# Layer 1's end in a new order, with biases over 128 rows and one-hot masks on GpSimd

## The chip, the cores and the metric

The kernel runs on one core of a Trainium2 chip. The metric is the device time of one execution in microseconds; a kernel is told by the median of its timed runs. Five engines work beside each other, each in the order of its own instructions: PE (TensorE, products into PSUM), ACT (ScalarE), DVE (VectorE), POOL (GpSimd) and SP (which issues DMAs). They wait for each other by semaphores.

## The reference, cut to what matters

Four transformer layers, each an attention and a feed-forward part, run on 4096 rows of 128 numbers, all in fp32; each part works on layer-normed rows and its output is added to the rows. The change lies in the feed-forward part of layer 1:

```python
x1 = x @ sw1.T + sb1;  x2 = x @ sw2.T + sb2            # x: layer-normed rows, 64 wide out
sh = _ln(silu(x1) * x2, s_ln_g, s_ln_b)
shared_out = sh @ sw3.T + sb3                           # 128 wide out
x_moe = x[index_b, index_t]                             # 256 chosen rows
shared_scores = sigmoid(x_moe @ sg_w.T + sg_b)
expert_scores = sigmoid(x_moe @ eg_w.T + eg_b)          # 8 experts
top1_idx = argmax(expert_scores + exp_bias, -1)
top1_score = take_along_axis(expert_scores, top1_idx[:, None], -1)
weights = softmax(concatenate([shared_scores, top1_score], -1), -1)
h1 = einsum('md,ehd->meh', x_moe, ew1) + eb1
h2 = einsum('md,ehd->meh', x_moe, ew2) + eb2
z = _ln(silu(h1) * h2, sel_ln_g, sel_ln_b)
out_all = einsum('meh,edh->med', z, ew3) + eb3
expert_out = take_along_axis(out_all, top1_idx[:, None, None], 1)[:, 0]
final_out = shared_out.at[index_b, index_t].set(
    shared_out[index_b, index_t] * weights[:, :1] + expert_out * weights[:, 1:])
x = x + final_out
```

So all 4096 rows go through a shared expert, and 256 chosen rows get a weighted mix of the shared expert and the best of eight experts instead. Layer 2's attention follows at once, on the layer norm of these rows.

## The kernel before, in words

The rows are held on the chip as eight batches `x[0]` to `x[7]` of 512 rows, each 128 partitions x 4 tiles x 128 columns. Within a layer the order of the instructions on every engine is the order in which the program issues them; layer 1 writes that order out by hand.

Layer 1 first runs a loop over the batches with a list of stages, each with its own lag (`stages`), which brings attention for all batches up to batch 7 and the shared expert for batches 0 and 1. Then comes a straight list of calls, the end of layer 1, which the change rewrites. Its steps, per batch b:

- `f_stats(b)` (L885): mean and variance of the four tiles by DVE, the reciprocal root by three small POOL instructions (`stats_of` L700, `rstd_` L240). `f_scale(b)` (L888): ACT writes the normed rows `fxn` (two buffers), and SP writes them to DRAM (`by_rows`). `f_turn(b)`: four PE transposes, an ACT copy to `fxt`.
- `f_product(b)` (L913): products with `sw12` by `by_token` (L248), which adds the bias as one more product of `ones`, a single row, with the bias; ACT takes the tanh; `t[b]["gated"]()` is the DVE rest of the gate, giving `z`. `f_gate(b)` is both.
- `z_stats`, `z_scale`, `z_turn`: layer norm of `z`, transposed into `zts[b % 2]`.
- `z_out(b)`: products with `sw3`, then four DVE multiply-adds into `x[b]` with the mask `rest` (0 for chosen rows). `z_out_by_three(b)` (L950) does the same by PE, ACT (`zo`, one buffer) and a POOL add.

The 256 chosen rows go beside it, as two groups m: `chosen_biases` (L965) starts two pairs of PSUM banks with the experts' biases; `chosen_rows` (L971) gathers the rows from `by_rows` with two indirect DMAs of POOL, once all `by_rows` are written; `chosen_products`, `chosen_gates` (best expert as a one-hot `one`), `chosen_select` (L1037, the gate for all experts, times the one-hot, summed over experts), `chosen_norm`, `chosen_scale`, `chosen_affine`, `chosen_mix`, `chosen_turn`, and `chosen_out` (L1103), which gives `val`. `chosen_back` (L1132) writes `val` to its rows of the DRAM tensor `back` (zero elsewhere) with two indirect DMAs; layer 2 adds `back` to batches 1 to 7 later. For batch 0 there is no time for that: `put_rows(0)` (L760) makes one-hot matrices of the chosen positions, and `chosen_put` multiplies them with `val` and adds the product to `x[0]`. Then `x[0]` is normed (`stats_of`, `scaled`, `turned`) into `xt`, on which layer 2 starts (`queries(0)` in `late`).

`keep_clock(n)` (L769) is n products of the identity with itself, into a bank that nobody reads. Layer 2's first instruction on DVE writes `qb` into memory that layer 1's tiles had. PSUM in layer 1 is four single banks (`bank`) and two double ones (`bank2`), used in turn.

## Time and profile before

| | us |
|---|---|
| median of three timed runs | 1488.48 |
| lowest, highest of them | 1482.74, 1493.97 |
| the profiled execution | 1480.14 |
| its span, first to last instruction | 1478.4 |
| PE busy | 1402.5 (95%) |
| ACT busy | 1048.4 (71%) |
| DVE busy | 981.8 (66%) |
| POOL busy | 646.2 (44%) |
| mean granted clock of PE | 0.986 |

A row of the profile names the source line, the engine, the operation and the tiles (output, then inputs), how often it occurred and how long it took; the bracket at its end is how long the engine stood idle before it and which instruction of which engine it then followed. In rows of the timeline the first number is the start, in us from the start of the span. A `by_token` product is on line 246 for PE, as all products share that helper. The end of layer 1 lies from about 465 us (the last gather of attention) to 534 us (layer 2's first queries).

### The profile page before, as it was taken

The numbers are of one execution on the slowest core, as the hardware profiler recorded it, in microseconds if no ns is written. First come the engines' busy times: TensorE is split into PE (matmuls) and PEld (weight loads), VectorE is DVE, ScalarE is ACT, GpSimd is POOL, SyncE is SP. The second block draws the span as 40 slices with busy tenths as digits, with TensorE's granted clock in tenths as the row PEclk, the third lists the DMA queues.
The fourth block names the chain that finished last, engine by engine and source line by source line (L and its number), as shares of the span: only waits on it lengthen the run. The fifth ranks groups of instructions, "written<-read, shape, count | busy, mean of one in ns | idle before, by whom it ended". The sixth has DMA issues, their size and how long they took to land.

```text
span 1478.4 us, 22290 instructions
## 1 busy us (share of the span) xinstructions
PE 1402.5 (95%) x7766; PEld 673.5 (46%) x7766; DVE 981.8 (66%) x2049; ACT 1048.4 (71%) x2145; POOL 646.2 (44%) x744
## 2 busy tenths in 40 slices
PE   7789999999889889999999999999999999999996
PEld 3652222222376554443443445444445454454465
DVE  6766655675376638642673487786786777877876
ACT  7859899999776546664865585776876867668632
POOL 6647666665564333310530162452442623514423
PEclk9999999999999889999999999999999999999999
DMA  4049999898431011001000000000000000000000
GB/s 170 1 61 128 135 131 129 128 126 116 124 97 30 11 34 29 27 11 29 1 1 1 1 1 8 1 1 8 1 0 8 1 8 1 0 8 0 2 8 15
DMA packets 32897, 58.91 MB, mean 40 GB/s; under 512 B 5521, under 2 KB 25553, under 8 KB 28306
## 3 DMA queue, kind: packets, MB, share of 16 engines
q1 hardware_dynamic: 32080, 55.66, 21.5%
q8 instruction: 62, 1.02, 0.3%
q10 hardware_dynamic: 578, 1.57, 0.3%
q14 instruction: 49, 0.40, 0.1%
q0 software_dynamic: 128, 0.26, 0.1%
HBM read 49.18 MB, written 8.29 MB: 39 GB/s over the span
## 4 chain that ended last, share of the span: by engine, by line
PE 70%; ACT 18%; DVE 8%; issue 1%; POOL 1%; DMA 1%; POOLq 0%; DVEq 0%; ACTq 0%
PE ps L246 68%; ACT hm L555 8%; ACT hm L554 4%; ACT ex L1440 2%; DVE nm L1434 1%; DVE s L707 1%; DMA gates<-eq 1%; ACT xn L1356 1%; PE ps L1770 1%; POOL rs L243 0%; ACT h L376 0%; ACT xn L718 0%; DVE x L262 0%; PE ps L933 0%; DVE pr L567 0%
## 5 line engine op out<-in xcount | busy, mean ns | idle before, releaser
L1440 ACT ACTIVATE ex<-ps,nm 128x512 f32<-128x512 f32 x512 | 346.1, 688 | 183.4 <-DVE nm L1434 181.6
L1434 DVE TENSOR_REDUCE nm<-ps 128x2 f32<-128x1024 f32 x256 | 300.6, 1216 | 62.0 <-PE ps L246 61.4
L246 PE MATMUL ps<-q,k 64*128 64x512 f32 x1024 | 258.4, 621 | 5.6 <-ACT ex L1440 4.8
L246 PE MATMUL ps<-ex,vs 128*64 128x512 f32 x1024 | 233.8, 598 | 0.0
L573 POOL TENSOR_TENSOR acc<-acc,pr 128x512 f32<-128x512 f32 x119 | 166.4, 1398 | 110.0 <-DVE pr L567 102.3
L1455 POOL TENSOR_TENSOR vs<-v,sm 128x256 f32<-128x256 f32 x128 | 81.3, 635 | 295.9 <-DVE sm L1454 278.3
L555 ACT ACTIVATE hm<-ps,blob_f 128x1536 f32<-128x1536 f32 x128 | 196.3, 1534 | 0.0
L246 PE MATMUL ps<-xt,blob_a 128*128 128x512 f32 x304 | 151.4, 624 | 0.0
L246 PE MATMUL ps<-h,w 32*128 32x512 f32 x1024 | 148.9, 643 | 2.3 <-ACT xt L742 0.8
L567 DVE SCALAR_TENSOR_TENSOR pr<-ps,blob_f,gs 128x512 f32<-128x512 f32 x120 | 90.1, 751 | 91.0 <-PE ps L246 74.3
L246 PEld LDWEIGHTS ps<-q,k 64*128 64x128 f32 x1024 | 87.6, 187 | 137.7 <-issue 70.4
L246 PE MATMUL ps<-hm,w 128*32 128x512 f32 x1024 | 137.1, 607 | 3.5 <-DVE pr L567 3.4
L246 PEld LDWEIGHTS ps<-ex,vs 128*64 128x64 f32 x1024 | 67.8, 136 | 148.5 <-issue 131.1
L1642 POOL TENSOR_TENSOR acs<-acs,prod 128x512 f32<-128x512 f32 x98 | 124.7, 1272 | 10.7 <-ACT prod L1641 6.2
L242 POOL TENSOR_SCALAR rs<-mv 128x4 f32<-128x4 f32 (+1 forms) x69 | 17.9, 260 | 201.4 <-DVE mv L1346 140.8
L1440 ACT ACTIVATION_READ_ACCUMULATOR ex<-ps,nm 128x1 f32 x512 | 104.8, 205 | 0.0
L554 ACT ACTIVATE hm<-ps,blob_f 128x512 f32<-128x512 f32 x128 | 88.0, 688 | 19.1 <-PE ps L246 19.0
L246 PEld LDWEIGHTS ps<-xt,blob_a 128*128 128x128 f32 x304 | 52.9, 192 | 87.0 <-issue 62.1
L246 PEld LDWEIGHTS ps<-h,w 32*128 32x128 f32 x1024 | 41.1, 183 | 111.1 <-ACT hm L554 94.4
L1402 DVE TENSOR_TENSOR v<-ps,blob_bc 128x512 f32<-128x512 f32 x64 | 44.3, 692 | 67.5 <-PE ps L246 43.0
L246 PEld LDWEIGHTS ps<-blob_a,ct 128*128 128x128 f32 x512 | 67.0, 191 | 32.3 <-issue 29.2
L243 POOL TENSOR_TENSOR rs<-rs,half 128x4 f32<-128x4 f32 (+1 forms) x69 | 72.6, 1052 | 5.8
(296 smaller groups left out, 2206.9 us busy)
## 6 DMA issues: line engine op xcount, KB each, us to landing
gs<-gates SPq DMA_DIRECT2D x256, 128.0 KB
blob_f<-in_f SPq DMA_DIRECT2D x1, 2560.0 KB
blob_a<-in_a SPq DMA_DIRECT2D x1, 2056.0 KB
x<-in_x SPq DMA_DIRECT2D x8, 256.0 KB
gates<-eq SPq DMA_DIRECT2D x8, 256.0 KB
by_rows<-fxn SPq DMA_DIRECT2D x8, 256.0 KB
ge<-gates SPq DMA_DIRECT2D x4, 512.0 KB
back<-nought SPq DMA_DIRECT2D x7, 256.0 KB
```

The lines of the kernel that those rows point to most:

```text
L242: nc.gpsimd.tensor_scalar(t, var, EPS, None, ALU.add)
L243: nc.gpsimd.tensor_tensor(t, t, half[:, : t.shape[-1]], ALU.pow)
L246: nc.tensor.matmul(out_, lhs, rhs, start=start, stop=stop)
L554: nc.scalar.activation(hm[:, 0, :], p1, AF.Gelu, bias=bias)
L555: nc.scalar.activation(hm[:, 1:, :], p3, AF.Gelu, bias=bias)
L567: nc.vector.scalar_tensor_tensor(pr, po, f0["b2"][:, e : e + 1], gs, ALU.add, ALU.mult)
L573: nc.gpsimd.tensor_tensor(acc[:, b, :], acc[:, b, :], pr, ALU.add)
L1402: nc.vector.tensor_tensor(v, pv, bias, ALU.add)
L1434: nc.vector.tensor_reduce(nm, ps, AX.X, ALU.max, negate=True)
L1440: nc.scalar.activation(ex[kt][:, i, :], ps[:, i, :], AF.Exp, bias=nm[:, i : i + 1], accum_out=sm[:, kt, i : i + 1],)
L1455: nc.gpsimd.tensor_tensor(vs[:, tiles, :, :], vs_[n][:, tiles, :].rearrange("p j (i n) -> p j i n", i=2), sm[:, tiles, :].unsqueeze(3).to_ ...
L1642: nc.gpsimd.tensor_tensor(t["acs"], t["acs"], p, ALU.add)
```

## The change

It does five things. The bias of `sw12` and the biases of the experts are multiplied with `top_row`, a 128 x 128 matrix with ones in its first row and zeros below, instead of the single row `ones`; the experts' biases are loaded onto all 128 partitions (`ebs`) for it. The last `f_scale` writes its four tiles to DRAM one by one. `put_rows` and the multiplication by the one-hot in `chosen_select` are done by POOL; one of the two `zte` copies is done by DVE. `z_out_by_three` returns its POOL add for a later call and has two `zo` buffers; batches 6 and 7 use `z_out` again and batch 2 `z_out_by_three`. And the straight list has a new order, in which the shared expert of batches 5 to 7 lies between the steps of the chosen rows, with one `keep_clock(4)` in place of four calls with 5, 8, 10 and 6.

```diff
-    def by_token(terms, bias, width=D, tiles=J):
+    def by_token(terms, bias, width=D, tiles=J, by=None):
...
-            mm(pv, ones, bias.unsqueeze(1).to_broadcast([1, tiles, width]), start=False, stop=True)
+            n = bias.shape[0]
+            mm(
+                pv,
+                ones if by is None else by,
+                bias.unsqueeze(1).to_broadcast([n, tiles, width]),
+                start=False,
+                stop=True,
+            )
...
             def f_scale(b):
-                scaled(t[b]["fxn"], x[b], t[b]["fby"], J)
-                nc.sync.dma_start(
-                    by_rows[b * TB : (b + 1) * TB, :].rearrange("(j p) d -> p j d", p=P), t[b]["fxn"]
-                )
+                n = 1 if b == NB - 1 else J
+                to = by_rows[b * TB : (b + 1) * TB, :].rearrange("(j p) d -> p j d", p=P)
+                for j in range(0, J, n):
+                    scaled(fxn, x[b], t[b]["fby"], j + n, j)
+                    nc.sync.dma_start(to[:, j : j + n, :], fxn[:, j : j + n, :])
...
-                zo = wp.tile([P, J, D], F32, tag="zo", name="zo", bufs=1)
+                zo = wp.tile([P, J, D], F32, tag="zo", name="zo")
...
-                nc.gpsimd.tensor_tensor(x[b], x[b], zo, ALU.add)
+                return lambda: nc.gpsimd.tensor_tensor(x[b], x[b], zo, ALU.add)
...
-                    for k, name in enumerate(("eb1", "eb2")):
-                        mm(c_["two"][m][:, k, :], ones, rows[name], stop=False)
+                    for k in range(2):
+                        mm(c_["two"][m][:, k, :], top_row, ebs[:, k, :], stop=False)
...
-            def chosen_select(m):
+            def chosen_select():
...
-                nc.vector.tensor_tensor(s3, s3, one, ALU.mult)
+                    nc.gpsimd.tensor_tensor(s3, s3, one, ALU.mult)
...
-                    nc.scalar.copy(zte, pt)
+                    (nc.vector.tensor_copy if m else nc.scalar.copy)(zte, pt)
...
+                nc.gpsimd.memset(top_row, 0.0)
+                nc.gpsimd.memset(top_row[:1, :], 1.0)
+                for k, name in enumerate(("eb1", "eb2")):
+                    lo, hi = spans["rows"][name]
+                    nc.sync.dma_start(ebs[:, k, :], dram["rows"][:, lo:hi].partition_broadcast(P))
```

The straight list after the change (where `chosen_out` is cut into `chosen_shared_out`, `chosen_products_out` and `chosen_out`, and `chosen_put` into its product and its addition; `addN` is the POOL add that `z_out_by_three` returned):

```python
gather(7) f_stats(5) output(6) z_scale(1) attend(7) f_stats(6) f_gate(2) turn_o(7) f_scale(5)
z_turn(1) output(7) f_stats(7) f_scale(6) f_turn(5) f_scale(7) z_out(1) z_stats(2)
put_rows(0, POOL) chosen_rows() chosen_biases() f_turn(6) f_gate(3) z_scale(2) z_stats(3) f_turn(7)
z_turn(2) f_gate(4) z_stats(4) chosen_products() chosen_gates() z_scale(3) add2 = z_out_by_three(2)
f_product(5) chosen_select() z_turn(3) add3 = z_out_by_three(3) chosen_shared() chosen_norm() add2()
z_scale(4) z_turn(4) add3() chosen_scale() t[5]["gated"]() z_stats(5) chosen_mix()
add4 = z_out_by_three(4) f_product(6) chosen_affine() chosen_turn() add4() chosen_shared_out()
t[6]["gated"]() chosen_products_out() z_stats(6) z_scale(5) z_turn(5) f_product(7) chosen_out()
chosen_put_product() z_scale(6) add5 = z_out_by_three(5) t[7]["gated"]() z_stats(7) chosen_put()
by = stats_of(x[0]) chosen_back() add5() z_turn(6) z_scale(7) z_out(6) z_turn(7) scaled(xn, x[0])
x[0] += lb (POOL) z_out(7) keep_clock(4) turned(xn)
```

and before:

```python
gather(7) f_stats(5) output(6) z_scale(1) attend(7) f_scale(5) f_stats(6) f_gate(2) turn_o(7)
z_turn(1) output(7) f_stats(7) f_scale(6) chosen_biases() f_scale(7) z_out(1) z_stats(2)
chosen_rows() f_turn(5) f_gate(3) f_turn(6) z_stats(3) z_scale(2) f_gate(4) z_turn(2) f_turn(7)
z_stats(4) f_gate(5) z_out(2) z_stats(5) chosen_products() chosen_gates() z_scale(3) z_turn(3)
chosen_select(0) f_product(6) z_out_by_three(3) z_scale(4) z_turn(4) chosen_select(1)
chosen_shared() chosen_norm() keep_clock(5) chosen_scale() z_out_by_three(4) t[6]["gated"]()
z_stats(6) f_product(7) chosen_mix() chosen_affine() keep_clock(8) chosen_turn() t[7]["gated"]()
z_scale(5) put_rows(0, DVE) z_turn(5) chosen_out() z_stats(7) z_scale(6) z_out_by_three(5)
chosen_put() by = stats_of(x[0]) chosen_back() z_turn(6) z_out_by_three(6) keep_clock(10)
scaled(xn, x[0]) x[0] += lb (POOL) keep_clock(6) turned(xn) z_scale(7) z_turn(7) z_out_by_three(7)
```

More of the change, by code (lines that the diff above doesn't have):

```diff
@@ L798, in layer1 @@
             zts = [once.tile([65, TB], F32, tag=f"zt{i}", name="zt") for i in range(3)]
+            top_row = once.tile([P, P], F32, tag="top_row", name="top_row")
+            ebs = once.tile([P, 2, TB], F32, tag="ebs", name="ebs")
             def exponential(tag, src, shape):
@@ L888, in f_scale @@
             def f_scale(b):
-                t[b]["fxn"] = wp.tile([P, J, D], F32, tag="fxn", name="fxn")
-                scaled(t[b]["fxn"], x[b], t[b]["fby"], J)
-                nc.sync.dma_start(
-                    by_rows[b * TB : (b + 1) * TB, :].rearrange("(j p) d -> p j d", p=P), t[b]["fxn"]
-                )
+                t[b]["fxn"] = fxn = wp.tile([P, J, D], F32, tag="fxn", name="fxn")
+                n = 1 if b == NB - 1 else J
[3 more added lines that the diff above has]
+                    nc.sync.dma_start(to[:, j : j + n, :], fxn[:, j : j + n, :])
             def f_turn(b):
@@ L914, in f_product @@
                 fxt = t[b]["fxt"]
-                pv = by_token([(lambda j: cols(fxt, j), l1["sw12"])], bc["sb12"][0:1, :])
+                pv = by_token([(lambda j: cols(fxt, j), l1["sw12"])], bc["sb12"], by=top_row)
                 t[b]["z"] = wp.tile([P, J, 64], F32, tag="z", name="z", bufs=4)
@@ L1003, in chosen_products @@
                 c_["zs"] = once.tile([P, 4, 64], F32, tag="zs", name="zs")
-                pz = by_token([(lambda j: cols(xm, j), l1["sw12"])], bc["sb12"][0:1, :], tiles=2)
+                pz = by_token([(lambda j: cols(xm, j), l1["sw12"])], bc["sb12"], tiles=2, by=top_row)
                 c_["gated"] = gated(c_["zs"][:, 2:, :], pz, 2)
@@ L1035, in chosen_shared @@
                 c_["gated"]()
-            def chosen_select(m):
-                two, s = c_["two"][m], c_["s", m]
-                nc.vector.scalar_tensor_tensor(s, s, 1.0, two[:, 0, :], ALU.add, ALU.mult)
-                nc.vector.scalar_tensor_tensor(s, s, 0.5, two[:, 1, :], ALU.mult, ALU.mult)
-                s3 = s.rearrange("p (e h) -> p e h", e=8)
-                one = c_["one"][:, m, :].unsqueeze(2).to_broadcast([P, 8, 64])
-                nc.vector.tensor_tensor(s3, s3, one, ALU.mult)
-                nc.vector.tensor_reduce(
-                    c_["zs"][:, m, :], s3.rearrange("p e h -> p h e"), AX.X, ALU.add
-                )
+            def chosen_select():
+                for m in range(2):
+                    two, s = c_["two"][m], c_["s", m]
+                    nc.vector.scalar_tensor_tensor(s, s, 1.0, two[:, 0, :], ALU.add, ALU.mult)
+                    nc.vector.scalar_tensor_tensor(s, s, 0.5, two[:, 1, :], ALU.mult, ALU.mult)
+                    s3 = s.rearrange("p (e h) -> p e h", e=8)
+                    one = c_["one"][:, m, :].unsqueeze(2).to_broadcast([P, 8, 64])
+                    nc.gpsimd.tensor_tensor(s3, s3, one, ALU.mult)
+                for m in range(2):
+                    s3 = c_["s", m].rearrange("p (e h) -> p h e", e=8)
+                    nc.vector.tensor_reduce(c_["zs"][:, m, :], s3, AX.X, ALU.add)
             def chosen_norm():
@@ L1099, in chosen_turn, with chosen_shared_out @@
                     zte = wp.tile([P, TB], F32, tag="zte", name="zte")
-                    nc.scalar.copy(zte, pt)
+                    (nc.vector.tensor_copy if m else nc.scalar.copy)(zte, pt)
                     pts.append(zte)
-            def chosen_out():
-                pts = c_["pts"]
+            def chosen_shared_out():
                 pv = by_token([(lambda j: cols(zts[2], j), l1["sw3"][:65])], None, tiles=2)
@@ L1109, in chosen_out, with chosen_products_out @@
                     )
-                po = bank()
+            def chosen_products_out():
+                pts = c_["pts"]
+                c_["po"] = po = bank()
                 for m in range(2):
@@ L1127, in chosen_out @@
                     )
-                nc.vector.tensor_tensor(
-                    val, val, po[:, : 2 * D].rearrange("p (m d) -> p m d", m=2), ALU.add
-                )
+            def chosen_out():
+                po = c_["po"][:, : 2 * D].rearrange("p (m d) -> p m d", m=2)
+                nc.vector.tensor_tensor(val, val, po, ALU.add)
             def chosen_back():
@@ L1136, in chosen_back, with chosen_put_product @@
                     )
+            def chosen_put_product():
+                c_["pv"] = put_product(c_["put"])
             def chosen_put():
-                scaled_add(0, put_product(c_["put"]), inv)
+                scaled_add(0, c_["pv"], inv)
             stages = (
@@ L1186, in layer1 @@
                 attend(7)
-                f_scale(5)
                 f_stats(6)
@@ L1190, in layer1 @@
                 turn_o(7)
+                f_scale(5)
                 z_turn(1)
@@ L1194, in layer1 @@
                 f_scale(6)
-                chosen_biases()
+                f_turn(5)
                 f_scale(7)
@@ L1198, in layer1 @@
                 z_stats(2)
+                c_["put"] = put_rows(0, wp, nc.gpsimd)
                 chosen_rows()
-                f_turn(5)
+                chosen_biases()
+                f_turn(6)
                 f_gate(3)
-                f_turn(6)
+                z_scale(2)
                 z_stats(3)
-                z_scale(2)
+                f_turn(7)
+                z_turn(2)
                 f_gate(4)
-                z_turn(2)
-                f_turn(7)
                 z_stats(4)
-                f_gate(5)
-                z_out(2)
-                z_stats(5)
                 chosen_products()
@@ L1214, in layer1 @@
                 z_scale(3)
+                add2 = z_out_by_three(2)
+                f_product(5)
+                chosen_select()
                 z_turn(3)
-                chosen_select(0)
-                f_product(6)
-                z_out_by_three(3)
+                add3 = z_out_by_three(3)
+                chosen_shared()
+                chosen_norm()
+                add2()
                 z_scale(4)
                 z_turn(4)
-                chosen_select(1)
-                chosen_shared()
-                chosen_norm()
-                keep_clock(5)
+                add3()
                 chosen_scale()
-                z_out_by_three(4)
+                t[5]["gated"]()
+                z_stats(5)
+                chosen_mix()
+                add4 = z_out_by_three(4)
+                f_product(6)
+                chosen_affine()
+                chosen_turn()
+                add4()
+                chosen_shared_out()
                 t[6]["gated"]()
+                chosen_products_out()
                 z_stats(6)
+                z_scale(5)
+                z_turn(5)
                 f_product(7)
-                chosen_mix()
-                chosen_affine()
-                keep_clock(8)
-                chosen_turn()
+                chosen_out()
+                chosen_put_product()
+                z_scale(6)
+                add5 = z_out_by_three(5)
                 t[7]["gated"]()
-                z_scale(5)
-                c_["put"] = put_rows(0, wp, nc.vector)
-                z_turn(5)
-                chosen_out()
                 z_stats(7)
-                z_scale(6)
-                z_out_by_three(5)
                 chosen_put()
@@ L1245, in layer1 @@
                 chosen_back()
+                add5()
                 z_turn(6)
-                z_out_by_three(6)
-                keep_clock(10)
+                z_scale(7)
+                z_out(6)
+                z_turn(7)
                 xn = norm.tile([P, J, D], F32, tag="xn", name="xn")
@@ L1253, in layer1 @@
                 )
-                keep_clock(6)
+                z_out(7)
+                keep_clock(4)
                 t[0]["next"] = turned(norm, "xt", xn)
-                z_scale(7)
-                z_turn(7)
-                z_out_by_three(7)
     I3 = 352
```

## The prediction

> **What bounds the kernel now.** I read the page's table of engines first (PE 95% of the span, the next one ACT at 71%), then the row of slices, to find where PE is not full, then five-microsecond windows with the granted clock, then the timeline of each engine in the stage that the change touches.

> ```profile
> PE   7789999999889889999999999999999999999996
> ...
> PEclk9999999999999889999999999999999999999999
> ```

> From about 590 us on PE is full at the full clock; that part is not touched. The eights between 370 and 555 us (37 us a slice) are layer 1, its start and its end. Every microsecond by which layer 1's end hands over earlier to layer 2 is therefore a microsecond of the whole. The windows of that end (columns: width; busy PE, PEld, DVE, ACT, POOL; granted clock; DMA):

> ```profile
> 475.00:480.00 5.00, 5.00 (x20) 3.26 (x19) 1.72 (x12) 0.54 (x2) 1.46 (x3) 0.79 0.20 57
> ...
> 490.00:495.00 5.00, 4.69 (x11) 2.46 (x12) 3.78 (x27) 0.81 (x3) 2.65 (x5) 0.66 0.00 0
> ...
> 505.00:510.00 5.00, 4.97 (x29) 4.66 (x29) 2.37 (x8) 3.18 (x9) 1.70 (x4) 0.66 0.01 3
> ...
> 530.00:535.00 5.00, 3.75 (x13) 2.60 (x14) 0.00 (x0) 2.43 (x7) 3.03 (x3) 0.75 0.05 16
> 535.00:540.00 5.00, 4.22 (x8) 1.49 (x8) 0.82 (x2) 1.41 (x4) 1.26 (x1) 0.50 0.33 110
> ```

> In quarter-microsecond windows the clock is 0.5 in 477.9-481.3, 491.6-495.0, 505.2-508.6 and 532.5-542.8: one, one, one and three times 3.4 us. What PE does there:

> ```profile
> 473.91 3.70 PE L246 MATMUL ps<-blob_rows,ones 1*128 1x512 f32 x8
> 477.54 1.76 PE L246 MATMUL ps<-blob_l,zt 65*128 65x128 f32 x8
> ...
> 491.17 5.84 PE L246 MATMUL ps<-blob_l,xm 128*128 128x512 f32 x12
> ...
> 511.27 1.95 PE L246 MATMUL ps<-blob_c 128*128 128x128 f32 x16
> ...
> 525.10 3.74 PE L246 MATMUL ps<-blob_c 128*128 128x128 f32 x32
> ...
> 532.45 2.03 PE L246 MATMUL ps<-blob_l,zt 65*128 65x128 f32 x8 [0.87 <-ACT zt L934]
> 534.27 3.62 PE L246 MATMUL ps<-xt,blob_a 128*128 128x512 f32 x4
> ```

> The first half-clock piece follows 3.7 us in which PE was never idle, but multiplied one row by 128 columns. The rows with `blob_c` are filler (keep_clock). The last row is layer 2's first queries, at half speed. And three waits outside PE:

> ```profile
> 480.33 1.65 ACT L718 ACTIVATE fxn<-x,nb,rs 128x128 f32<-128x128 f32 x4 [4.79 <-PE ps L740]
> ```
> ```profile
> 485.43 1.23 POOL L974 DMA_INDIRECT row<-by_rows,at_int  x1 [2.39 <-issue]
> ```
> ```profile
> 537.09 0.17 DVE L2057 TENSOR_SCALAR qb<-blob_a 128x8 f32<-128x8 f32 x1 [11.77 <-POOL x L960]
> ```

> The last normed batch waits for PE, the gather of chosen rows waits for that batch in DRAM, and layer 2's first VectorE instruction waits for layer 1's last GpSimd add, since its tile lies in layer 1's memory.

> **Biases over 128 rows.** The instructions stay as many and as wide (eight of 512 columns, 3.57 us back to back either way). [...] By the row it was throttled straight after, so active rows count. By the row the change removes the first piece (half of 3.4 us with PE back to back: 1.7 us) and probably the second: its window before, 488.2-491.6, holds 1-row and 65-row products, transposes and a gap of 0.46, and twelve products took 5.84 us where 8 x 0.446 + 4 x 0.112 = 4.0 would do (1.8). I take the row: 3.5 us. Lower end 0, if 127 rows of zero weights don't count. The two loads of eb1 and eb2 onto 128 partitions add 0.5 MB on SP's queue ahead of the zero rows, near 398 us. The DMA engines run at 320-450 GB/s there, are done by 418, and by_rows starts at 424.6: 1.5 us, hidden; uncovered it would be 1.5.

> **The rows to DRAM.** f_turn(5) goes ahead of the biases and of z_out(1), so the last f_scale no longer waits 4.79 us. It then waits for its own statistics (POOL's nb ends at 477.7): 477.7-479.3 instead of 480.33-481.98. Before, the gather began 3.4 us after the issue of the last DMA (482.00 to 485.43), whose packets ended 1.9 after it. By tiles the last one carries 64 KB instead of 256; I take 2.7 us (3.4 at most, 2.4 at least, since only packet time shrinks). SP issues four at 0.4 us instead of one; nothing stands behind them. Rows complete for POOL at about 482.1.

> **Masks on POOL.** put_rows moves from DVE (2 x 0.44 at 512.4, off the path) to POOL just ahead of the gather. No POOL compare is in the trace. The nearest row, POOL TENSOR_SCALAR 128x512 (ex), takes 1.50 us; the fused two-scalar form on POOL (L336, 478 ns for 128 columns) would give 1.9. [...] By the row it runs 479.6-482.6 and delays the gather by 0.5. I take the row[...]. Rows then land at 482.6 + 1.53 + 2.5 = 486.7, against 489.5: **2.8 us earlier**. The statistics of z(3) and z(4) queue behind the gather, but are not asked for before 492.
> In chosen_select the multiplication by the one-hot goes to POOL: 1.27-1.40 instead of 0.69. Before, DVE took 495.26-501.47 (6.2). Now DVE does 4 x 0.72, the masks follow, the second ends near 4.2, two reductions of 0.95 end at 5.3: 0.9 saved though POOL is twice as slow.

> **The order.** PE does f_product(5) and z_out(2), 3.1 us, after the products instead of before. z_out(2) now goes by ACT and POOL (1.14 + 1.26), z_out(6) and z_out(7) by DVE (1.13 each), so the last POOL add, which ended at 537.06 and let qb go, is gone; the POOL adds are issued later than their zo (a second buffer), so that none stands ahead of the statistics of the chosen tokens. Chosen tokens: products end near 492.5 (497.6 before), select and norm give nb at 500.9; ACT, now with zo(2), zo(3), zn(4) and zt(4) ahead, starts znc at 501.6 (506.90 before): 5.3 earlier. Then ze ends 504.4, PE z_out(4), f_product(6) to 507, transposes and the DVE/ACT pair of zte to 509, products (2.3) to 511.5, z_turn(5), f_product(7) 2.05, put_product 1.8: done at 515.8 against 522.8. **7.0 earlier**: before, keep_clock(8), f_product(7) and z_turn(5) stood between ze (509.6) and products (517). 25 of 29 filler products go (25 x 0.223 = 5.6 us of PE).
> From put_product to the queries before took 11.4 us (522.8 to 534.27). Now: x0's sum and statistics 4 us plus 0.7 behind z_stats(7), to 520.5; ACT does zt(7) first, xn 521-522.6; z_out(7), keep_clock(4), four transposes and the copy to xt (0.59, now bare: before it lay under z_turn(7)) reach 526.8. 11.0 us. So queries begin at 526.8 instead of 534.27: 7.5 earlier, including the clock of the first two pieces.
> The wait of qb moves too. chosen_back holds POOL 3.6 us (the second indirect write starts 2.65 after the first), and add5, which frees layer 1's memory, queues behind: 520.5 + 3.6 + 1.27 = 525.5. That is earlier than K needs it (528), so it is hidden by 2 us now; if PE came warm and sooner it would bind.
> The clock of the end: the last stretch is still sparse (z_turn, z_out, gaps of about 1), with 4 fillers instead of 16. I expect half clock for the queries again, but two windows rather than three: 1 us more.

> **The sum.** 7.5 + 1 = 8.5. The same laying of rows end to end over before's own order reaches 531 where the trace has 534.3: it runs 3 us short. So 5.5. Profiled execution 1480.14 (span 1478.4): 1474.6. The median of the three timed runs is 8.3 above that execution (1482.7 to 1494.0). I read this as the windows falling unluckily in this sparse stage and elsewhere; the part in this stage should shrink, as fewer windows are near the edge. I leave 1 us for the rest: **1475.5**, 13 below the median, 0.9%.

> **Rivals.**
> (a) *Forecast*, 1475.5, own range 1471-1480: 0.47.
> (b) *The clock holds to the end*: for it, fewer 1-row products and shorter gaps. The end is then set by qb: scores start about 526.6 against 538.67, 12, and the first scores lose 1.8 us of half clock: 14 off the profiled 1480.1: 1466. Against it: keep_clock(4) is 0.9 us in a 3.4 us window. 0.25.
> (c) *Rows of zeros don't count, and the removed filler is missed*: the 3.5 us of clock come back, and one or two more windows go half while PE is on the path (1.7 each). Of 5.5 nothing remains, but the dear phases of before don't vanish either: about 1484. For it: 4 fillers where 29 were. 0.22.
> (d) *Slower*: the compare on POOL is slow. [...] The gather stands behind both masks, and all chosen work behind the gather. The loss is 1:1 beyond 1.5 each: [...]at 10 each +17. It is slower than the median of before from 8 us each (13 / 2 beyond 1.5); at 10 the time is 1492. 0.06.

> **Numbers.** Range 1465 to 1485: (a), most of (b) and (c). A change of 1% (15 us) is about what a measurement of this kernel can tell. Below 1473.6: (b) with 0.25 and a third of (a): 0.42. Above 1503: 0.03, from the far end of (d). The rest 0.55.

> **What would show it.** Right: no half clock after the biases; the transposes of the gathered rows near 487; znc near 502; put_product done near 516; queries near 527; qb waiting for POOL less than 1 us. POOL put rows at 1.5 each. Wrong: half clock straight after the 128-row biases (c), POOL masks above 3 us (d), queries after 531, or scores held by qb while Q is ready (b).

## The result, and the profile after

The changed kernel took 1475.4 us in the median of seven runs (1473.25 to 1477.91), beside 1488.48 for the kernel before (seven runs, 1482.53 to 1493.97): ratio 0.992, 95% interval 0.989 to 0.995. Thirteen more runs of it, among the experiments, gave 1478.19 (1472.38 to 1480.71; ratio 0.994, 0.991 to 0.996); all twenty have a median of 1477.1. The kernel before, in four such series, had medians of 1484.5 to 1488.5. So the gain is 6 to 13 us by series, somewhat under 1%. The profiled execution of the kernel after took 1477.4 us (span 1475.6), only 2.7 less than the profiled one before. The forecast was a sum over one profile, the result is told in medians, and this case turns on the difference.

The page's slices of the kernel after, in the two rows that were shown of before:

```profile
PE   7789999999889889999999999999999999999997
...
PEclk9999999999899889999999999999999999999998
```

Layer 1's end still has its eights, and the clock row is no better than before. The five-microsecond windows of the kernel after (width; busy PE, PEld, DVE, ACT, POOL; granted clock; DMA):

```profile
475.00:480.00 5.00, 4.61 (x25) 3.13 (x25) 4.45 (x24) 4.29 (x11) 2.70 (x5) 1.00 0.31 89
490.00:495.00 5.00, 4.48 (x10) 2.79 (x11) 2.03 (x14) 0.56 (x2) 1.65 (x4) 0.50 0.00 0
505.00:510.00 5.00, 2.84 (x12) 1.98 (x13) 4.54 (x16) 4.11 (x12) 4.76 (x7) 0.70 0.00 0
530.00:535.00 5.00, 4.32 (x14) 2.91 (x14) 1.81 (x5) 0.59 (x1) 3.46 (x3) 0.50 0.29 85
535.00:540.00 5.00, 4.22 (x14) 1.40 (x13) 1.86 (x2) 0.69 (x1) 0.00 (x0) 0.73 0.43 149
```

The clock of 475 to 480 went from 0.79 to 1.00. That of 490 to 495 fell from 0.66 to 0.50, and in 505 to 510 PE is idle for 2.2 us where before it was full. PE's timeline of the kernel after tells what stands there:

```profile
477.98 3.60 PE L246 MATMUL ps<-ebs,top_row 128*128 128x512 f32 x8
...
481.86 1.06 PE L246 MATMUL ps<-blob_l,fxt 128*128 128x128 f32 x8
...
488.86 0.30 PE L995 MATMUL ps<-blob_c,row 128*128 128x128 f32 x1 [1.24 <-DMA row<-by_rows,at_int]
490.05 0.48 PE L995 MATMUL ps<-blob_c,row 128*128 128x128 f32 x1 [0.88 <-DMA row<-by_rows,at_int]
...
492.49 6.23 PE L246 MATMUL ps<-blob_l,xm 128*128 128x512 f32 x12
...
508.37 0.59 PE L1079 MATMUL ps<-blob_c,pick 128*8 128x128 f32 x2 [1.24 <-DVE pick L1074]
...
529.71 1.92 PE L246 MATMUL ps<-blob_c 128*128 128x128 f32 x8
531.41 1.06 PE L748 MATMUL ps<-blob_c,xn 128*128 128x128 f32 x4
533.15 3.78 PE L246 MATMUL ps<-xt,blob_a 128*128 128x512 f32 x4 [0.68 <-ACT xt L750]
```

The biases run at full clock, and the eight products soon after them take 1.06, as elsewhere at full clock. But PE now waits for the gathered rows (1.24 and 0.88), where before it had f_gate(5) and z_out(2) to do; the experts' products behind the wait are at half clock (6.23), as they were before (5.84). The filler keep_clock(4) takes 1.92 at half clock in front of the turn of x0, and the queries are at half clock again. The record of the granted clock has 0.5 in 489.9-496.7, 507.0-513.8 and 527.4-537.7.

What fed those waits, on POOL, ACT and DVE of the kernel after:

```profile
481.88 4.01 POOL L772 TENSOR_SCALAR put<-blob_c,at_col 128x512 f32<-128x512 f32 x2
486.08 1.23 POOL L987 DMA_INDIRECT row<-by_rows,at_int  x1 [0.19 <-DVE mv L717]
...
498.43 1.04 POOL L1058 TENSOR_TENSOR se<-se,one 128x512 f32<-128x512 f32 x1 [6.54 <-DVE se L1055]
...
505.60 2.48 POOL L973 TENSOR_TENSOR x<-x,zo 128x512 f32<-128x512 f32 x2
```
```profile
479.66 1.66 ACT L726 ACTIVATE fxn<-x,nb,rs 128x128 f32<-128x128 f32 x4 [0.71 <-POOL nb L720]
```
```profile
505.79 1.10 DVE L718 TENSOR_SCALAR nb<-mv 128x4 f32<-128x4 f32 x1
506.80 0.16 DVE L1071 TENSOR_SCALAR mix<-score 128x2 f32<-128x2 f32 x1
506.87 1.24 DVE L1072 TENSOR_SCALAR mix<-score 128x2 f32<-128x2 f32 x1
...
532.79 0.73 DVE L2086 TENSOR_SCALAR qb<-blob_a 128x8 f32<-128x8 f32 x1 [1.71 <-POOL x L973]
```

f_scale(7) waits 0.71 instead of 4.79. The put masks take 2.0 each and the gather stands behind them. The two additions of zo lie at 505.60 to 508.08, and two DVE instructions on a few columns, 0.17 elsewhere, last 1.10 and 1.24 beside them; the pick, and PE behind it, wait for these. qb's wait fell from 11.77 to 1.71.

### The profile page after: what moved, and what is told of

Read it like the earlier page. It is cut to its first block, busy times and chain, and to the rows that moved or that the text cites. A ratio compares the mean times of both kernels' runs of the same rounds, so it can differ in the third digit from the quotient of the medians.

```text
span 1475.6 us, 22195 instructions
## 1 busy us (share of the span) xinstructions
PE 1396.4 (95%) x7716; PEld 670.2 (45%) x7716; DVE 982.0 (67%) x2050; ACT 1047.2 (71%) x2140; POOL 652.3 (44%) x749
## 4 chain that ended last, share of the span: by engine, by line
PE 69%; ACT 14%; DVE 9%; DMA 5%; issue 1%; POOL 1%; POOLq 0%; DVEq 0%; SPq 0%; ACTq 0%
PE ps L246 66%; ACT hm L563 6%; DMA gs<-gates 4%; ACT hm L562 3%; ACT ex L1469 2%; DMA gates<-eq 1%; DVE s L715 1%; DVE nm L1463 1%; ACT xn L1385 1%; PE ps L1799 1%; ACT xn L726 1%; POOL rs L243 0%; DVE pr L575 0%; ACT h L384 0%; DVE x L270 0%
## 5 line engine op out<-in xcount | busy, mean ns | idle before, releaser
L246 PE MATMUL ps<-q,k 64*128 64x512 f32 x1024 | 256.9, 617 | 5.7 <-ACT ex L1469 4.9
L246 PE MATMUL ps<-ex,vs 128*64 128x512 f32 x1024 | 233.8, 598 | 0.0
L246 PE MATMUL ps<-xt,blob_a 128*128 128x512 f32 x304 | 152.3, 627 | 0.7 <-ACT xt L750 0.7
L246 PE MATMUL ps<-h,w 32*128 32x512 f32 x1024 | 148.0, 639 | 2.3 <-ACT xt L750 0.8
L246 PEld LDWEIGHTS ps<-q,k 64*128 64x128 f32 x1024 | 87.0, 185 | 137.5 <-issue 69.9
L246 PE MATMUL ps<-hm,w 128*32 128x512 f32 x1024 | 137.1, 607 | 4.5 <-DVE pr L575 3.8
L246 PEld LDWEIGHTS ps<-ex,vs 128*64 128x64 f32 x1024 | 67.8, 136 | 148.5 <-issue 130.8
L562 ACT ACTIVATE hm<-ps,blob_f 128x512 f32<-128x512 f32 x128 | 88.2, 689 | 18.1 <-PE ps L246 18.0
L246 PEld LDWEIGHTS ps<-xt,blob_a 128*128 128x128 f32 x304 | 53.0, 193 | 88.6 <-issue 62.6
L246 PEld LDWEIGHTS ps<-h,w 32*128 32x128 f32 x1024 | 40.9, 183 | 110.3 <-ACT hm L562 93.7
L246 PEld LDWEIGHTS ps<-blob_a,ct 128*128 128x128 f32 x512 | 67.0, 191 | 32.3 <-issue 29.2
```

What stands on the lines that cost most here:

```text
L246: nc.tensor.matmul(out_, lhs, rhs, start=start, stop=stop)
L562: nc.scalar.activation(hm[:, 0, :], p1, AF.Gelu, bias=bias)
```

## The experiments

Two stretches of a trace are compared throughout: from the first product of the last gather of attention, gather(7), to layer 2's first context product (ps<-ex,vs), called **the stage**; and from there to the end of the span. The second is 924.8 to 925.2 us in all fourteen profiles, so layer 2 onwards is never touched. gather(7) itself starts anywhere from 464.9 to 468.1, in kernels that are alike up to there.

| kernel | median us (runs) | ratio to before, interval | stage | of it half clock | half clock in the stage, profiled run |
|---|---|---|---|---|---|
| before | 1488.48 (7) | | 88.2 | 20.5 | 477.9-481.3, 491.6-495.0, 505.2-508.6, 532.5-542.8 |
| after | 1475.4 (7) | 0.992 (0.989-0.995) | 82.7 | 23.9 | 489.9-496.7, 507.0-513.8, 527.4-537.7 |
| e1 before, 128-row biases | 1476.47 (6) | 0.993 (0.990-0.995) | 82.8 | 10.2 | 489.6-493.0, 503.2-506.7, 530.6-534.0 |
| e7 before, 64 rows | 1480.46 (20) | 0.9965 (0.995-0.998) | 85.7 | 13.7 | 492.4-499.2, 509.5-512.9, 536.8-540.2 |
| e8 before, 32 rows | 1484.05 (20) | 0.999 (0.997-1.0005) | 85.8 | 13.7 | 492.0-498.9, 509.1-512.5, 536.4-539.8 |
| e11 before, experts' biases only | 1481.56 (22) | 0.997 (0.995-0.9985) | 86.2 | 17.1 | 490.0-493.4, 503.6-507.0, 530.9-541.2 |
| e2 after, 1-row biases | 1481.51 (9) | 0.998 (0.995-1.001) | 84.2 | 27.3 | 479.8-483.2, 490.0-493.4, 503.7-520.7, 531.0-534.4 |
| e3 after, put masks late | 1474.44 (6) | 0.9905 (0.988-0.993) | 83.1 | 23.9 | 491.3-494.8, 505.0-511.8, 525.5-539.1 |
| e4 after, one-hot on DVE | 1477.17 (6) | 0.993 (0.990-0.995) | 83.0 | 23.9 | 488.5-495.4, 505.6-512.4, 526.1-536.3 |
| e5 after, no filler | 1472.53 (6) | 0.9925 (0.990-0.995) | 79.7 | 17.1 | 490.1-493.5, 503.8-510.6, 524.2-531.1 |
| e6 after, wait filled | 1473.42 (6) | 0.993 (0.990-0.995) | 79.6 | 20.5 | 498.9-509.2, 522.8-533.1 |
| e9 after, three edits | 1470.66 (6) | 0.990 (0.986-0.994) | 78.9 | 20.5 | 499.5-506.3, 520.0-533.6 |
| e10 the three and f_product(6) | 1473.56 (7) | 0.992 (0.988-0.995) | 79.5 | 23.9 | 498.6-505.4, 508.8-512.2, 522.5-536.1 |
| e12 after again | 1478.19 (13) | 0.994 (0.991-0.996) | 82.7 | 23.9 | 489.3-496.1, 506.4-513.2, 526.8-537.1 |

The kernel before scatters most (1477 to 1494), so the ratios carry its noise; e1 to e4 share one series of it (median 1488.28), e5 to e8 another (1484.6), e9 to e12 a third (1484.45). The first and the third are from the same chip, so a gain against before is uncertain by some 4 us from series to series. e5 to e8 ran on a second chip; the kernel after was not run there.

**Theories.** T1: rows of zero weights count for TensorE's clock, and this is the gain. T2: the gain is the new order's. To begin with, the two were taken apart crosswise.

### e1: the old order with the new biases

```diff
# in the kernel before
-                    for k, name in enumerate(("eb1", "eb2")):
-                        mm(c_["two"][m][:, k, :], ones, rows[name], stop=False)
+                    for k in range(2):
+                        mm(c_["two"][m][:, k, :], top_row, ebs[:, k, :], stop=False)
...
-                pv = by_token([...], bc["sb12"][0:1, :])
+                pv = by_token([...], bc["sb12"], by=top_row)
```

> The order of before, with one part of the change alone: all sw12 biases and the experts' biases over 128 rows. If active rows count for the clock: no half clock straight after the experts' biases, two pieces of 3.4 us fewer near 478 and 492, 3 to 6 us below before, and less scatter. If rows of zero weights don't count[...]: the same half-clock pieces as before and the same time within 1 us. If the whole gain of the change is clock: all of 13 us.

1476.47: 11.8 below before in the same series (7.6 to 14.3 by the interval), about as much as the whole change brought. PE's timeline:

```profile
473.92 3.60 PE L246 MATMUL ps<-ebs,top_row 128*128 128x512 f32 x8
477.35 1.06 PE L246 MATMUL ps<-blob_l,zt 65*128 65x128 f32 x8
...
487.92 0.33 PE L991 MATMUL ps<-blob_c,row 128*128 128x128 f32 x1 [0.76 <-DMA row<-by_rows,at_int]
...
489.58 5.83 PE L246 MATMUL ps<-blob_l,xm 128*128 128x512 f32 x12
```

The products behind the biases take 1.06, where they took 1.76. So rows of zeros count, and the first half of T1 holds. In median, what the order adds to it cannot be told from nothing.

But the two kernels got there by different ways. The stage of e1 is as short as that of the kernel after (82.8 beside 82.7). In e1 half clock fell from 20.5 to 10.2 us, and half of that difference, 5.1, is nearly all that the stage lost (5.4). In the kernel after half clock rose to 23.9, and the stage lost 5.5 all the same. An estimate from the traces: PE is busy at half clock for 19.7 us of the stage in before, 10.2 in e1, 20.2 in after and 26.3 in e2; less half of that, the stages are 78.3, 77.7, 72.6 and 71.0. By this the new order is some 6 us shorter at full clock, and it leaves PE emptier (idle 12.9 us of the stage instead of 10.3), so that the clock doesn't gain there. The mean granted clock, which is on record for every run, agrees: its median is 0.980 in before and 0.990 in e1, in the same series, but 0.982 in the twenty runs of the kernel after.

### e2: the new order with the old biases

```diff
-                        mm(c_["two"][m][:, k, :], top_row, ebs[:, k, :], stop=False)
+                        mm(c_["two"][m][:, k, :], top_row[:1], ebs[:1, k, :], stop=False)
# and bc["sb12"][:1], by=top_row[:1] in f_product and chosen_products
```

> The changed kernel with all these biases over one row again (order, masks and DMAs by tile stay). If rows count: half clock comes after the 3.6 us of experts' biases, 3 to 6 us above the changed kernel, about 1480. If the order alone brings the gain: 1475, as the changed kernel.

1481.51, with single runs from 1476.77 to 1493.47. PE's timeline of this kernel:

```profile
476.20 3.69 PE L246 MATMUL ps<-ebs,top_row 1*128 1x512 f32 x8
...
480.74 1.92 PE L246 MATMUL ps<-blob_l,fxt 128*128 128x128 f32 x8
```

The half clock straight after the one-row biases is back: eight products that take 1.06 in the kernel with 128 rows take 1.92. The wide scatter is back with it. Its profiled execution, 1476.77, is the fastest of its runs; none of 1493 was profiled. But the mean granted clock falls with the time, from 0.983 in the fastest run to 0.969 in the slowest: 0.014 of 1480 us are 21 us of clock, and the runs lie 16.7 apart. So the scatter goes with the clock. The order alone is worth 6.8 us between the medians (1488.28 to 1481.51); the interval goes from 8.0 faster to 1.0 slower.

### e7, e8: how many rows

```diff
-                        mm(c_["two"][m][:, k, :], top_row, ebs[:, k, :], stop=False)
+                        mm(c_["two"][m][:, k, :], top_row[:64], ebs[:64, k, :], stop=False)
# in the kernel of e1; the shared biases likewise; e8 with 32
```

> The kernel before with the biases multiplied over 64 rows instead of 1 (63 of them with zero weights), where the same over 128 rows took 1476.5. If the clock follows the share of TensorE's rows in use, 64 rows count about half: some of the half-clock windows stay, and the time is between 1478 and 1486. If it is enough that the rows are not one (any sizeable number counts as busy), 1476 to 1477.5. If only all 128 rows count, 1487 to 1489.

> As the 64-row kernel, with 32 rows. If the clock follows the share of rows in use, 32 rows are nearly as bad as one: 1484 to 1489. If any sizeable number of rows counts as busy: 1476 to 1478.

1480.46 and 1484.05. With 1 and 128 rows the ratios make a ladder: 1, 0.999, 0.9965, 0.993 for 1, 32, 64 and 128 rows. A loss in proportion to the rows left out would give 0.998 and 0.996 for 32 and 64. By these medians the clock follows the share of rows in use; neither "more than one row" nor "all or nothing" fits (e1 is of another series than e7 and e8). e7 and e8 have all that e1 has but the rows, the loads and tiles of `ebs` and `top_row` too: so it is not by these that e1 gains.

### e11: which biases

```diff
# in the kernel of e1
-                pv = by_token([...], bc["sb12"], by=top_row)
+                pv = by_token([...], bc["sb12"][0:1, :])
# and the same in chosen_products
```

> The kernel before with only the four biases of the routed experts (8 entries of 512 columns, 3.6 us in one piece) multiplied over 128 rows, and the biases of the shared experts' products over 1 row as before. If the one long piece near 478 is what lowers the clock, this gives the whole gain of the biases: 1476 to 1478. If the short pieces count as well (1.0 us in each f_product, between full work), part of the gain is left out: 1479 to 1485.

1481.56: about 3 of the gain come with the experts' biases, whose 3.6 us in one piece were the visible culprit. PE's timeline shows that piece mended, and the shared biases at one row still between full products:

```profile
474.29 3.60 PE L246 MATMUL ps<-ebs,top_row 128*128 128x512 f32 x8
...
480.05 1.12 PE L246 MATMUL ps<-blob_bc,ones 1*128 1x512 f32 x2
```

The rest, more than half, comes with the short pieces of 1.1 us, one in each f_product. They don't empty a window of 3.4 us, but they take a third of it away, and the windows of this stretch are not far from the edge: by the count of the last section those of before from 471.1, 481.3 and 498.4 hold 0.45, 0.46 and 0.41, where half clock followed up to 0.39.

### e3, e4: the POOL masks

```diff
# e3
-                c_["put"] = put_rows(0, wp, nc.gpsimd)
                 chosen_rows()
+                c_["put"] = put_rows(0, wp, nc.gpsimd)
# e4
-                    nc.gpsimd.tensor_tensor(s3, s3, one, ALU.mult)
+                    nc.vector.tensor_tensor(s3, s3, one, ALU.mult)
```

> The changed kernel with the two one-hot masks issued behind the two gathers on GpSimd instead of ahead. The masks took 4.0 us for the pair, not the 3.0 of my sum, and the gather began at 486.1 right behind them, though the last rows were written to DRAM from 481.4. If they hold up the gather: it starts some 2 us earlier, PE's waits for the rows (1.24 and 0.88 us) go, and with them perhaps the two half-clock pieces over the products: 2 to 5 us below the changed kernel. If the DMA's landing decides: no change.

> The changed kernel with the multiplication by the one-hot in chosen_select on VectorE as before (put rows stay on GpSimd). By my sum GpSimd saves 0.9 us on the way to the norm: 1 us above the changed kernel. By the rival, that a two-input product on GpSimd is twice as slow and only adds a hand-over: 1 us below.

e3 gave 1474.44 and e4 1477.17, neither to be told from the kernel after by their medians. In e3's trace POOL is free, and the gather waits for the rows in DRAM instead:

```profile
485.13 1.23 POOL L987 DMA_INDIRECT row<-by_rows,at_int  x1 [3.98 <-DMA by_rows<-fxn]
```

The last tile's DMA had been issued at 480.82: 4.31 us to the gather, where one DMA of 256 KB had taken 3.43 before. Against gather(7) the gather begins at 18.2, and in the kernel after at 18.4. So the masks cost nothing here, because the DMA by tile is as late as they are.

### e5: no filler ahead of x0's turn

```diff
-                keep_clock(4)
```

> The kernel after without keep_clock(4), the filler of 1.92 us at half clock that stands on TensorE between z_out(7) and the turn of x0's scaled rows. If the filler stands on the path (xn was ready at 529.34, the turn began only at 531.5), the layer-2 start comes 1.5 to 2 us earlier after gather(7) than the 82.7 us of the kernel after, and the time is about 1473.5. If the filler earns a clock window for the queries of block 0, taking it away costs what it saves, and the time stays within 1 us of 1475.4. The windows that follow should stay at half clock in both, since the filler is too short to fill one.

1472.53. Of the six runs five are below 1474, against six of the twenty of the kernel after; the stage is 3.1 shorter. PE goes from z_out(7) straight to the turn:

```profile
524.57 2.08 PE L246 MATMUL ps<-blob_l,zt 65*128 65x128 f32 x8 [0.86 <-ACT zt L946]
526.44 1.06 PE L748 MATMUL ps<-blob_c,xn 128*128 128x128 f32 x4
528.17 3.40 PE L246 MATMUL ps<-xt,blob_a 128*128 128x512 f32 x4 [0.68 <-ACT xt L750]
```

1.7 of the 3.1 are the filler's; the rest are windows that fell otherwise (the products at 5.84 instead of 6.23, the queries at 3.40). The filler came after the fall and couldn't undo it.

### e6: work in the wait for the rows

```diff
+                add2 = z_out_by_three(2)
+                f_product(5)
                 chosen_products()
                 chosen_gates()
                 z_scale(3)
-                add2 = z_out_by_three(2)
-                f_product(5)
```

> The kernel after with z_out_by_three(2) and f_product(5) moved ahead of chosen_products, so that TensorE has work while it waits for the gathered rows (idle 1.24 and 0.88 us plus the half-clock pieces near 490 in the kernel after). If the idle time of TensorE ahead of the rows is what puts the products of the routed experts at half clock (6.23 us for 12), they run at full clock (about 3.5 us), znc comes 2 to 4 us earlier against gather(7), and the time is 1472 to 1474. Rival: the moved work delays the products by as much as it saves, because f_product(5)'s evictions on ScalarE stand ahead of chosen_products' Tanh: then within 1 us of 1475.4.

1473.42, all six runs below 1475, and the stage 3.1 shorter. PE's timeline:

```profile
489.02 0.38 PE L995 MATMUL ps<-blob_c,row 128*128 128x128 f32 x2
...
490.78 4.15 PE L246 MATMUL ps<-blob_l,xm 128*128 128x512 f32 x12
...
496.15 1.29 PE L945 MATMUL ps<-blob_c,zn 128*64 128x128 f32 x4 [0.79 <-ACT zn L726]
498.31 1.55 PE L246 MATMUL ps<-blob_l,zt 65*128 65x128 f32 x8 [0.87 <-ACT zt L946]
```

PE no longer waits for the rows, and the twelve products take 4.15: full clock. It is this wait that had put them at half clock. The next fall came at 498.9, after PE had stood idle again ahead of the turn of zn(3) (0.79) and behind it (0.87).

### e9, e10, e12: together, and after again

```diff
# e9: e5 and e6, and POOL's additions behind the mixture
-                add2()
                 z_scale(4)
                 z_turn(4)
-                add3()
                 chosen_scale()
                 t[5]["gated"]()
                 z_stats(5)
                 chosen_mix()
+                add2()
+                add3()
# e10: as e9, and
                 z_scale(4)
+                f_product(6)
                 z_turn(4)
...
-                f_product(6)
```

> The kernel after with three edits at once: the work moved into TensorE's wait for the rows and the filler left out, which alone gave 1473.4 and 1472.5, and GpSimd's two additions of zo (2.48 us) issued after the gates' mixture on VectorE instead of before it. With the additions late, the two small VectorE operations (L718 and L1072) that took 1.03 and 1.24 us beside them should take 0.17 each again and the pick comes about 2 us earlier. If the three gains add up: 2.0 + 2.9 + 1 to 2 below after, so 1469 to 1470. If the clock windows decide and the gains overlap (the queries are at half clock in either case): 1471 to 1473.

> As the kernel with three edits, and f_product(6) (2.1 us of TensorE at full clock) moved up between z_turn(3) and z_turn(4), where TensorE stood idle 1.56 and 1.75 us and then fell to half clock for 10.2 us in the kernel with the rows' wait filled. If the idle pieces there cause that fall, the half clock near 499 to 509 shortens by one or two windows and the time falls by 1 to 3 us against the kernel with three edits. Rival: one such piece of work is too little for a window of 3.4 us, or its eviction delays ScalarE's zt and znc: no change within 1 us, or 1 us slower.

> The kernel after itself, unchanged, on the same chip as the kernels with three and four edits, so that they are compared with it directly: 1474 to 1477 if the chip is like the one before; the kernels with three and four edits should lie 3 us or more below it if their gains are real.

e9 took 1470.66 (five of six runs 1470.1 to 1472.3), 7.5 below the kernel after in the same series; those five lie below the lowest of the thirteen runs of the kernel after (1472.38). It is the fastest version of this study, and beats both kernels. Its PE at layer 2's start, and its DVE with POOL beside it:

```profile
524.18 3.78 PE L246 MATMUL ps<-xt,blob_a 128*128 128x512 f32 x4 [0.68 <-ACT xt L750]
528.74 2.08 PE L246 MATMUL ps<-q,k 64*128 64x512 f32 x4 [0.78 <-ACT q L1440]
```

```profile
500.35 0.17 DVE L718 TENSOR_SCALAR nb<-mv 128x4 f32<-128x4 f32 x1
500.43 0.18 DVE L1071 TENSOR_SCALAR mix<-score 128x2 f32<-128x2 f32 x1
500.53 0.15 DVE L1072 TENSOR_SCALAR mix<-score 128x2 f32<-128x2 f32 x1
...
502.23 2.48 DVE L1090 TENSOR_TENSOR znc<-znc,blob_bc 128x128 f32<-128x128 f32 x2 [1.34 <-ACT znc L726]
504.74 2.36 DVE L1103 TENSOR_TENSOR ze<-znc,pick 128x512 f32<-128x512 f32 x2
```
```profile
502.02 2.54 POOL L973 TENSOR_TENSOR x<-x,zo 128x512 f32<-128x512 f32 x2
505.01 1.55 POOL L973 TENSOR_TENSOR x<-x,zo 128x512 f32<-128x512 f32 x1 [0.45 <-ACT zo L970]
```

The small instructions are back at 0.17 and PE waits 0.22 for the pick, but znc and ze now lie beside the additions and take 2.48 and 2.36 instead of 0.62 and 1.29. PE doesn't wait for ze, as f_product(6) keeps it busy at half clock until then. Against gather(7) the pick reaches PE 1.9 earlier than in e6, and ze 1.3 earlier. To put the additions behind ze as well would need a third zo buffer and wasn't tried.

By the stages e5 and e6 save 3.1 each, and e9 only 3.9. Up to layer 2's queries, though, the savings add up: these start 65.5 us after gather(7) in the kernel after, at 62.8 in e5, 62.3 in e6 and 59.3 in e9. The rest is lost behind them. In e9 half clock lasts for 9.4 us after the queries' start (to 533.6), in the kernel after for 4.5, so in e9 the scores run at half clock as well (four in 2.08), and the first context comes 19.6 us after the queries instead of 17.2.

e10 brought nothing on top: 1473.56 (1469.71 to 1477.19). PE's timeline:

```profile
498.62 2.08 PE L246 MATMUL ps<-blob_l,zt 65*128 65x128 f32 x8 [0.86 <-ACT zt L946]
500.49 1.91 PE L246 MATMUL ps<-blob_l,fxt 128*128 128x128 f32 x8
502.19 1.91 PE L246 MATMUL ps<-blob_bc,top_row 128*128 128x512 f32 x2
503.90 1.06 PE L945 MATMUL ps<-blob_c,zn 128*64 128x128 f32 x4
```

The clock had already fallen at 498.6, behind a sparse window (PE idle for 0.79 and 0.86 of its 3.4 us). So it was in e6: the idle 1.56 and 1.75 us that the expectation took for the cause ended at 501.42 and 504.57, behind the fall at 498.9. The product comes after the fall and runs at half speed, 3.4 us from 500.49 to 503.90, about as long as in its old place (3.1 in e9), with z_turn(4) now queued behind it; and one more window went half, at 508.8. By e6 and e10 it is the window before the fall that has to be filled: work ahead of the fall kept the clock for the twelve products (4.15 in e6 instead of 6.23), and work behind it ran at half clock itself (1.91 for the eight in e10).

## Why the prediction was right, and where it was not

The forecast, 1475.5, was met to 0.1 us by the first series of runs and to 1.6 by all twenty. That rows count is shown. The sum behind the forecast is not: several terms were wrong, and they cancelled, so that the closeness is luck in good part.

- **Rows count for the clock: right** (the products behind the biases took 1.06 in e1, 1.76 in before), and in e1 worth more than was said (5.4 in the stage). Forecast were 3.5 us in the profile, by two pieces. The first piece went in every kernel with 32 rows or more in the profiled run. The second, on the experts' products, did not go by the rows: it stays in e1 and after, where PE waits for the gathered rows ahead of it (0.76; 1.24 and 0.88), and went when that wait was filled (e6). And the kernel after has more half clock in its stage than before (23.9 beside 20.5), not less: what its profiled run gained came in the main by the shorter order (e2, with one-row biases, already has 4.0 of the 5.5), not by the clock. By the prediction's lower end, at which rows of zero weights don't count, e1 would have been worth 0; it was worth 11.8.
- **From the profile to the median: the term that was most mis-sized.** The prediction left 1 us for the 8.3 by which the median of before stood above its profiled run. In fact the medians fell by 13.1 where the profiles fell by 2.7. The reading of the 8.3 as windows that fall unluckily agrees with e1, e7 and e8, where the rows alone lower the median in steps. It agrees with the mean granted clock too: in the 92 runs of before that stand beside the experiments it is 0.987 and 0.988 in the two fastest (1477.3 and 1477.5) and 0.976 in the two slowest (both 1494.4). Which windows the longer runs lose is not shown, since none of them was profiled. The profiled run of the kernel after came out 2.8 above its forecast of 1474.6, and the first median 2.0 below that run instead of 1 above the forecast one: the two errors cancel.
- **The rows to DRAM: half right.** The wait of 4.79 went, as said. "By tiles I take 2.7 us" from the last issue to the gather was wrong: 4.31 in e3. The put masks took 2.0 each instead of 1.5; the trace's row of the fused form, by which the prediction gave 1.9, was the nearer one. The gather began 18.4 us after gather(7), which is 486.08 less 467.68, against 17.5 as forecast (482.6 less 465.15). In before it was 20.3, and in e1, with the old order and one DMA, 18.7: most of this gain is the biases' too. The second group of rows reached PE 2.0 earlier than before (22.4 against 24.4 after gather(7)), not 2.8.
- **The one-hot product on POOL:** 1.04 each, not 1.27 to 1.40. e4 without it has a stage 0.3 longer: its forecast gain of 0.9 can't be seen.
- **The order: the step that failed.** znc was to be 5.3 earlier and put_product 7.0. Against gather(7), znc on ACT starts at 40.2 instead of 41.8, 1.6 earlier, and put_product at 52.9 instead of 55.7, 2.8 earlier. The walk laid f_product(5) and z_out(2) behind the products and let the rows be there when PE came; they were not, and the products, taken at full clock, ran at half. It also let POOL's additions go beside DVE for nothing, which cost the pick 2.0 (1.10 and 1.24 instead of 0.17 each). "The same walk over before's order runs 3 short" stood for all this unnamed, and happened to be its size: 7.5 + 1 - 3 = 5.5, and the stage did shrink by 88.2 - 82.7 = 5.5. But 2.5 of it went to gather(7), which started later (467.68 instead of 465.15) for windows that fell otherwise ahead of the change.
- **The end:** half clock for the queries, as said, but for three windows and not two. The stage's tail, from the queries (69.1 and 65.5 after gather(7)) to the first context, fell all the same from 19.1 to 17.2, as the queries start nearer to those windows' end: 1.8, where 1 was said. The filler, costed at 0.9, lasted 1.92 at half clock and took 1.7 of the path (e5).
- **qb:** said to wait less than 1 us; it waited 1.71, and ended before K needed it. Not on the path, as said.
- **Rivals.** The clock that holds to the end did not come about in any kernel here. The slow compare did not either (2.0 each, where more than 3 would have shown it). Rows that don't count is refuted by e1; that rival's other half, that more windows go half where the filler was, did come about (23.9 us of half clock in the stage for 20.5). The absolute marks (queries near 527, put_product done near 516) were missed by 6, of which 2.5 is gather(7)'s.

## What to carry to other kernels

Feed TensorE whole partitions even where the algebra needs one: a bias as a 128-row product with zero weights took no more time than with one row (eight in 3.60 and 3.70), and kept the clock (the eight products behind it took 1.06 in e1, 1.76 in before). A shorter path can cost clock: the new order took, by the estimate under e1, some 6 us of work and waits away, left PE emptier (idle 12.9 us of the stage instead of 10.3), and had no less half clock than before (23.9 beside 20.5), so look at both. Read the clock's cause in the window before the fall, and put work there (e6: 4.15 instead of 6.23); the filler after the fall only cost (1.7 in e5). When a profile of one execution is the base of a forecast, look first at where that execution lies among the runs: a change that takes away bad luck is seen in the median and hardly in the profile.
